# The layer norm's subtract-and-scale on GpSimd instead of VectorE, in a four-layer fp32 attention kernel

## Chip, cores and metric

One Trainium2 chip, one core. The metric is the device time of one execution in microseconds (us). Everything is fp32.

## What is computed

The input x has 8 sequences of 112 rows of 256 values (896 rows); the context has 8 sequences of 375 rows of 192. Four layers follow on each other, ten stages in all:

- L0 and L1: self-attention (16 heads of 64), cross-attention to the context (16 heads of 64), and a gated feed-forward of inner width 1024.
- L2: one cross-attention (16 heads of 64).
- L3: causal self-attention (16 heads of 16), cross-attention (16 heads of 16), feed-forward.

Ahead of each stage stands a layer norm, and after it a residual sum:

```python
def _layer_norm(x, g, b):
    m = jnp.mean(x, axis=-1, keepdims=True)
    v = jnp.mean(jnp.square(x - m), axis=-1, keepdims=True)
    return (x - m) * jax.lax.rsqrt(v + EPS) * g + b
...
h = _layer_norm(x, g, b); x = x + stage(h) @ Wo + bo
```

There are ten norms over 896 rows. The part `(x - m) * rsqrt(v + EPS)` is what the change moves; `g` and `b` are applied later, when the transposed result is copied out of PSUM.

## The kernel before

The residual x lies in SBUF as seven tiles of 128 rows by 256 (`x_sb`; the profile merges them as `x`, and a norm's result as `xn`). The work on TensorE (PE) is cut into items with a cost and a due time. A planner (class `Plan`) emits them one after the other: the attention steps are the backbone, and projections, output products, transposes of normed tiles and feed-forward blocks are filled in between by due time. PE's order is written out by this planner and is kept as it is (`manual_schedule` for PE alone). The other engines' orders are set by the tile framework from the same program; each engine runs its own queue in order, so that an instruction that waits holds all that is behind it.

An attention step s (function `add_step`) does for four heads (cross) or eight or sixteen (self):

1. `emit_s`: scores on PE into PSUM (L818).
2. `softmax`: in L3's self-attention VectorE (DVE) adds the causal mask (L777); DVE takes the row maximum with a minus sign (`nm`, L783; L787 caps it in L3); ScalarE (ACT) takes exponentials and their sums (`pr`, L793); DVE takes the reciprocal (`rinv`, L799 and L803); GpSimd (POOL) multiplies `pr` by it (L800 for each cross-attention head, 112x375; L804 for eight self-attention heads at once, 112x896).
3. `emit_t`: PE transposes `pr` (L837), and a copy takes it out of PSUM into `wT`.
4. `emit_pv`: PE multiplies `wT` with the values (L857), and a copy brings the result into `oT`.

The order in PE's queue is scores of step i+2, values product of step i, then the transposes of step i+1 with filler items between them.

Copies out of PSUM go through `evac` (L299 to L303 on ACT, L307 to L311 on DVE). It keeps a running load of ACT and of DVE and gives each copy to the one that would be done first; `busy(engine, us)` adds to this load what other instructions take. It changes which engine copies, not PE's order. PSUM has four buffers for these tiles (`mm`), and PE waits for a copy where all four are held.

The output product of a stage (`add_products`) ends with DVE adding PSUM to the residual tile (L553), after which `norm` is called at once for the next stage:

- DVE: `bn_stats` (L498), `bn_aggr` (L500, mean and variance into `mv`), the variance plus EPS (`ve`, L502).
- POOL: `ve` to the power -0.5, giving `rs` (L504, 128x1).
- DVE: `xn = (x - mean) * rs` (L506, 128x256).
- POOL: the next stage's bias row is added to the residual tile (L507, 128x256), once xn has read it.

The small tiles `st`, `mv`, `ve` and `rs` have four buffers each and xn has three; a buffer is free again when its last reader is done. Some time later PE transposes xn (L520, function `add_norm_transposes`), for tiles two at a time, and two copies apply `g` and `b`.

`norm` is called 70 times: seven at the start of the program, and 63 times spread over the other stages. What else is in POOL's queue: at the start the memset of `brows`, a DMA into it (L344), its scaling (L345) and a memset (L346), which PE's transpose of `brows` (L349) waits for; near the end of L2 the context mask (`ctxB`, L481, 1x3000) and memsets of padded weights (L426, L434, L444, L454); in L3 memsets of the spread value tiles (L624), which DVE then fills (L625). The sync engine's queue (SP) issues the loads of weights and rows.

Of the kernel before, what the change touches and what calls it, by code (L numbers as in the profile page):

```python
# [12 lines left out]
ALU = mybir.AluOpType  # L13
# [249 lines left out]
def kernel(ctx: ExitStack, tc: tile.TileContext, a: dict, out: bass.AP):  # L263
    nc = tc.nc
# [23 lines left out]
    def busy(eng, us):  # L288
        load[eng] = max(load[eng], plan.now) + us
# [27 lines left out]
    for t in range(NT):  # L317
        xt = const.tile([P, D], F32, name=f"x{t}")
# [176 lines left out]
    def norm(st, t):  # L495
        xt = x_sb[t]
        s6 = small.tile([P, 6], F32, tag="st", name="st")
        nc.vector.bn_stats(s6, xt)  # L498
        mv = small.tile([P, 2], F32, tag="mv", name="mv")
        nc.vector.bn_aggr(mv, s6)  # L500
        ve = small.tile([P, 1], F32, tag="ve", name="ve")
        nc.vector.tensor_scalar_add(ve, mv[:, 1:2], EPS)  # L502
        rs = small.tile([P, 1], F32, tag="rs", name="rs")
        nc.gpsimd.tensor_tensor(rs, ve, mhalf, ALU.pow)  # L504
        xn = xpool.tile([P, D], F32, tag="xn", name="xn")
        nc.vector.tensor_scalar(xn, xt, mv[:, 0:1], rs, ALU.subtract, ALU.mult)  # L506
        nc.gpsimd.tensor_add(xt, xt, got[("row", st)])  # L507
        busy("dve", 1.3)
        xns[(st, t)] = xn

    def add_norm_transposes(st, g, bt, deadline, first=False):
# [29 lines left out]
    def add_products(st, nxt, w, n, after, deadline):  # L541


        for t in range(NT):

            def fn(t=t):
                ps = mm_tile()
                for c in range(n):
                    nc.tensor.matmul(  # L549
                        ps[:, :D], lhsT=oT[:, c, t * P : (t + 1) * P], rhs=got[w][:, c, :],  # L550
                        start=(c == 0), stop=(c == n - 1),
                    )
                nc.vector.tensor_add(x_sb[t], ps[:, :D], x_sb[t])  # L553
                busy("dve", 0.42)
                if nxt is None:
                    nc.sync.dma_start(oflat[t * P : (t + 1) * P, :], x_sb[t])
                else:
                    norm(nxt, t)

            plan.add(  # L560
                Item(
                    ("out", t) if nxt is None else ("norm", nxt, t), n * 0.43, fn, deadline(t),
                    uses=[w] + ([] if nxt is None else [("row", nxt)]), deps=after(t),
                    seg=SEG[st] + (info[st][0] == "ff"),
                )
            )
# [591 lines left out]
    for t in range(NT):  # L1158
        norm(0, t)
        plan.refs[("row", 0)] = plan.refs.get(("row", 0), 0)  # L1160
        plan.ev[("norm", 0, t)] = 1.0
# [67 lines left out]
```

## Time before, and its profile

| | us |
|---|---|
| median of 3 runs | 1764.25 |
| lowest and highest run | 1763.3 and 1764.34 |
| the profiled execution's own time | 1763.93 |
| its span | 1762.1 |
| PE busy in the span | 1698.7 |
| POOL busy | 821.6 |
| DVE busy | 894.7 |
| ACT busy | 760.4 |
| xn on DVE (L506), 70 instructions, median of one | 0.412 |
| rs on POOL (L504), 70 instructions, median of one | 0.567 |
| row add on POOL (L507), 70 instructions, median of one | 0.726 |
| DVE idle ahead of xn until rs came, in total | 71.1 |

A profile is of one execution. A line of its timeline reads: start in us from the span's start, duration, engine, line of the kernel, operation, output<-input, shape, count; in square brackets the time that the engine stood idle before it and the instruction whose end released it. PE is the matrix engine, PEld its weight loads, which overlap PE. A line of the table by stage gives for each stretch of the span the busy time of the engines, and in brackets the number of instructions. A wait for several events is put down to the one that came last.

The stretches that matter below: 0 to 20 us is the start (x is loaded, the first norm, its transposes); up to about 1080 run L0 and L1, up to about 1397 L2, up to about 1485 L3's self-attention, up to about 1706 L3's cross-attention, and the rest is L3's feed-forward. The borders overlap, since each stage's projections and the last products of the one before are filled in between steps.

### The profile page before, as it was taken

What the parts mean: (1) busy time and instruction counts of PE and PEld (TensorE: products, weight loads), DVE (VectorE), ACT (ScalarE), POOL (GpSimd) and SP (SyncE); (2) the same over time, 40 slices, a digit from 0 to 9 for tenths busy, and PEclk for the clock granted to TensorE, in tenths of its full rate; (3) what the DMA queues carried; (4) which work ended last, traced back from release to release, by engine and by line L of the source; (5) the groups of instructions that cost most, each with busy time, mean ns of one, the idle gap of its engine ahead of it and who ended that gap; (6) DMA issues with size and microseconds to landing.
All of it is one profiled execution on the core that took longest, in us unless ns stands there. A gap on an engine that the chain in (4) does not pass through costs nothing.

```text
span 1762.1 us, 30334 instructions
## 1 busy us (share of the span) xinstructions
PE 1698.7 (96%) x11886; PEld 1187.1 (67%) x11886; DVE 894.7 (51%) x2106; ACT 760.4 (43%) x2420; POOL 821.6 (47%) x755
## 2 busy tenths in 40 slices
PE   6999999999999999999999999999999888999979
PEld 5777666666658876666666657766656776666656
DVE  2454455455522445555455523555555477666640
ACT  3553344444412444344444421444444356555541
POOL 3212545455601222555455602645657535788860
PEclk9999999999999999999999999999999999999999
DMA  6012011000101110000000100100000101000000
GB/s 182 4 48 52 3 29 54 25 1 1 49 28 42 28 49 25 1 28 1 25 1 1 43 27 9 10 1 1 7 1 7 11 14 50 2 1 1 1 1 22
DMA packets 39464, 39.12 MB, mean 22 GB/s; under 512 B 16928, under 2 KB 34568, under 8 KB 39321
## 3 DMA queue, kind: packets, MB, share of 16 engines
q1 hardware_dynamic: 39257, 37.13, 7.6%
q8 instruction: 94, 1.54, 0.4%
q14 instruction: 49, 0.40, 0.1%
q0 software_dynamic: 64, 0.05, 0.0%
HBM read 35.48 MB, written 0.92 MB: 21 GB/s over the span
## 4 chain that ended last, share of the span: by engine, by line
PE 85%; DVE 5%; POOL 4%; ACT 4%; issue 1%; DMA 0%; SPq 0%; ACTq 0%; POOLq 0%; DVEq 0%
PE mm L581 11%; PE mm L549 11%; PE mm L837 9%; PE s L818 9%; PE mm L857 9%; PE mm L677 7%; PE mm L1030 7%; PE mm L643 7%; PE mm L686 4%; PE mm L652 4%; PE mm L605 3%; ACT pr L793 3%; POOL pr L800 3%; DVE nm L783 2%; PE mm L707 1%; PE mm L728 1%
## 5 line engine op out<-in xcount | busy, mean ns | idle before, releaser
L800 POOL TENSOR_SCALAR pr<-pr,rinv 112x375 f32<-112x375 f32 x512 | 623.9, 1238 | 400.3 <-DVE rinv L799 394.1
L793 ACT ACTIVATE pr<-s,nm 112x375 f32<-112x375 f32 (+1 forms) x768 | 374.2, 503 | 260.9 <-DVE nm L783 171.5
L783 DVE TENSOR_REDUCE nm<-s 112x2 f32<-112x750 f32 (+1 forms) x288 | 266.1, 952 | 63.9 <-PE s L818 59.8
L837 PE MATMUL mm<-ident,pr 112*128 112x112 f32 (+2 forms) x1920 | 240.9, 264 | 17.8 <-DVE oT L311 5.9
L837 PEld LDWEIGHTS mm<-ident,pr 112*128 112x128 f32 (+2 forms) x1920 | 213.3, 151 | 64.1 <-issue 15.7
L303 ACT COPY wT<-mm 128x448 f32<-128x448 f32 (+2 forms) x292 | 153.0, 535 | 179.1 <-PE mm L837 178.6
L857 PEld LDWEIGHTS mm<-wT,v 128*64 128x64 f32 (+5 forms) x3840 | 161.7, 130 | 94.1 <-issue 33.6
L857 PE MATMUL mm<-wT,v 128*64 128x112 f32 (+5 forms) x3840 | 202.4, 266 | 15.7 <-ACT wT L303 12.3
L818 PE MATMUL s<-kT,qT 64*112 64x375 f32 (+3 forms) x1792 | 208.6, 394 | 0.0
L804 POOL TENSOR_TENSOR pr<-pr,rinv 112x896 f32<-112x896 f32 x48 | 80.8, 1684 | 267.9 <-DVE rinv L803 248.0
L818 PEld LDWEIGHTS s<-kT,qT 64*112 64x112 f32 (+1 forms) x1792 | 113.5, 173 | 68.3 <-issue 15.6
L793 ACT ACTIVATION_READ_ACCUMULATOR pr<-s,nm 112x1 f32 x768 | 158.3, 206 | 0.0
L799 DVE RECIPROCAL rinv<-sums 112x1 f32<-112x1 f32 x512 | 83.1, 162 | 98.6 <-ACT pr L793 88.4
L311 DVE COPY kT<-mm 128x375 f32<-128x375 f32 (+1 forms) x117 | 65.6, 561 | 119.0 <-PE mm L652 99.9
L311 DVE COPY wT<-mm 128x448 f32<-128x448 f32 (+2 forms) x188 | 114.2, 611 | 14.0 <-PE mm L837 11.0
L311 DVE COPY v<-mm 128x512 f32<-128x512 f32 (+2 forms) x75 | 51.8, 691 | 130.2 <-PE mm L686 109.5
L303 ACT COPY kT<-mm 128x375 f32<-128x375 f32 (+1 forms) x107 | 51.2, 478 | 128.3 <-PE mm L652 115.2
L504 POOL TENSOR_TENSOR rs<-ve,mhalf 128x1 f32<-128x1 f32 x70 | 39.2, 561 | 143.9 <-DVE ve L502 142.0
L553 DVE TENSOR_TENSOR x<-mm,x 128x256 f32<-128x256 f32 x70 | 29.4, 419 | 128.7 <-PE mm L549 128.6
L643 PE MATMUL mm<-ctxA,L_xattn_Wk 128*128 128x375 f32 x256 | 91.7, 480 | 0.0
L677 PE MATMUL mm<-L_xattn_Wv,ctxA 128*128 128x512 f32 (+1 forms) x192 | 90.7, 595 | 0.4 <-ACT hT L299 0.4
L303 ACT COPY v<-mm 128x512 f32<-128x512 f32 (+2 forms) x53 | 31.1, 586 | 125.6 <-PE mm L686 120.4
(130 smaller groups left out, 2342.2 us busy)
## 6 DMA issues: line engine op xcount, KB each, us to landing
L_xattn_Wq<-in_L_xattn_Wq_dram SPq DMA_DIRECT2D x3, 1024.0 KB, 6.8
L_xattn_Wo<-in_L_xattn_Wo_dram SPq DMA_DIRECT2D x3, 1024.0 KB, 15.2
L_xattn_w_ff<-in_L_xattn_w_ff_dram SPq DMA_DIRECT2D x3, 1024.0 KB, 5.7
L_xattn_Wp<-in_L_xattn_Wp_dram SPq DMA_DIRECT2D x2, 1024.0 KB, 7.5
L_xattn_wq<-in_L_xattn_wq_dram SPq DMA_DIRECT2D x2, 1024.0 KB, 4.9
L_xattn_wo<-in_L_xattn_wo_dram SPq DMA_DIRECT2D x2, 1024.0 KB, 5.8
L_xattn_mlp_w<-in_L_xattn_mlp_w_dram SPq DMA_DIRECT2D x2, 1024.0 KB, 4.9
cn<-in_ctx_dram SPq DMA_DIRECT2D x2, 843.8 KB
```

The lines of the kernel that those rows point to most:

```text
L303: nc.scalar.copy(dst, src)
L311: nc.vector.tensor_copy(dst, src)
L549: nc.tensor.matmul(ps[:, :D], lhsT=oT[:, c, t * P : (t + 1) * P], rhs=got[w][:, c, :], start=(c == 0), stop=(c == n - 1),)
L581: nc.tensor.matmul(ps[:, i * 2 * T : (i + 1) * 2 * T], lhsT=got[w][:, k, m * P : (m + 1) * P], rhs=hT[:, k, lo:hi], start=(k == 0), stop=( ...
L643: nc.tensor.matmul(ps[:, :S], lhsT=got[w][:, (2 * u + i) * P : (2 * u + i + 1) * P], rhs=ctxA[:, cols], start=True, stop=False,)
L677: nc.tensor.matmul(ps[: KCH[c][1], :], lhsT=lhs(ctxA, slice(0, KA), c), rhs=got[w][:, hf * 512 : (hf + 1) * 512], start=True, stop=False,)
L783: nc.vector.tensor_reduce(nm[:, :, :ns], sv, AX.X, ALU.max, negate=True)
L793: nc.scalar.activation(pr[:, bk, sl, :], sv[:, bk, sl, :], AF.Exp, bias=nm[:, bk, sl : sl + 1], accum_out=sums[:, bk, sl : sl + 1],)
L800: nc.gpsimd.tensor_scalar_mul(pr[:, bk, sl, :], pr[:, bk, sl, :], rinv[:, bk, sl : sl + 1])
L818: nc.tensor.matmul(tiles[i][:, n % 2, (n // 2) * nk : (n // 2 + 1) * nk], lhsT=qap(h), rhs=kap(h), start=True, stop=True,)
L837: nc.tensor.transpose(pt[:kl, i * T : (i + 1) * T], cell[h][:, c * P : c * P + kl], ident[:T, :T])
L857: nc.tensor.matmul(po[p0 : p0 + dp, blk * T : (blk + 1) * T], lhsT=got[vk][:kl, hv * dp : (hv + 1) * dp], rhs=wt, start=(c == 0), stop=(c ...
```

## The change

The instruction that makes xn is issued on GpSimd's queue, between the power that gives `rs` and the row add, instead of on VectorE's. The load figure that `evac` is told for a norm's instructions on VectorE goes from 1.3 to 0.8. Nothing else is edited.

```diff
@@ -503,9 +503,9 @@
         rs = small.tile([P, 1], F32, tag="rs", name="rs")
         nc.gpsimd.tensor_tensor(rs, ve, mhalf, ALU.pow)
         xn = xpool.tile([P, D], F32, tag="xn", name="xn")
-        nc.vector.tensor_scalar(xn, xt, mv[:, 0:1], rs, ALU.subtract, ALU.mult)
+        nc.gpsimd.tensor_scalar(xn, xt, mv[:, 0:1], rs, ALU.subtract, ALU.mult)
         nc.gpsimd.tensor_add(xt, xt, got[("row", st)])
-        busy("dve", 1.3)
+        busy("dve", 0.8)
         xns[(st, t)] = xn
```

In the built program 70 instructions move from VectorE's queue to GpSimd's. PE's queue and SP's keep their order. Ten of some 1300 copies out of PSUM go to VectorE instead of ScalarE.

## The prediction

> **What bounds the kernel now.** I read part 1 of the page, then the busy time by stage, then the waits of VectorE (DVE) and of TensorE (PE), and last the timeline wherever PE stands still.
>
> ```profile
> PE 1698.7 (96%) x11886; PEld 1187.1 (67%) x11886; DVE 894.7 (51%) x2106; ACT 760.4 (43%) x2420; POOL 821.6 (47%) x755
> ```
>
> PE is the bound: it idles 63 us of a span of 1762.1. The stages show where (start:end, then length, PE, weight loads, DVE, ACT, POOL, clock, DMA):
>
> ```profile
> 0.00:40.00 40.00, 25.00 (x123) 21.45 (x124) 9.73 (x33) 12.86 (x34) 11.54 (x26) 1.00 0.62 183
> ...
> 20.00:1355.00 1335.00, 1330.00 (x8765) 914.42 (x8764) 647.73 (x1445) 552.64 (x1725) 568.37 (x495) 1.00 0.08 22
> 1355.00:1397.00 42.00, 36.64 (x264) 29.77 (x266) 18.30 (x51) 14.18 (x39) 30.87 (x30) 0.96 0.18 12
> 1397.00:1485.00 88.00, 77.14 (x813) 63.83 (x806) 69.99 (x150) 52.27 (x261) 32.68 (x35) 0.96 0.10 30
> 1485.00:1706.00 221.00, 197.21 (x1820) 138.41 (x1817) 144.16 (x415) 124.69 (x370) 176.17 (x168) 0.98 0.01 2
> ```
>
> From 20 to 1355 us PE idles 5 us in all: whatever VectorE loses there on GpSimd (POOL) is hidden. Time can be won or lost in the first 20 us, and in block L3 from 1355 to 1706, where PE idles 40 us (5.4 + 10.9 + 23.8).
>
> The wait that the change aims at is this one, of DVE (total, times, longest):
>
> ```profile
> DVE xn L506 <- POOL rs L504: 71.1, 60, 8.5
> ```
>
> Of it, 39.3 us in 19 waits lie after 1355. The worst, and a usual one in the cross attention of L3:
>
> ```profile
> 1357.66 7.78 POOL L481 TENSOR_SCALAR ctxB<-c 1x3000 f32<-1x3000 uint8 x1 [0.17 <-POOL x L507]
> ...
> 1373.32 0.57 POOL L504 TENSOR_TENSOR rs<-ve,mhalf 128x1 f32<-128x1 f32 x1
> 1373.93 0.41 DVE L506 TENSOR_SCALAR xn<-x,mv,rs 128x256 f32<-128x256 f32 x1 [8.52 <-POOL rs L504]
> ...
> 1375.66 1.76 PE L857 MATMUL mm<-wT,v 119*64 119x112 f32 x16 [5.36 <-ACT wT L303]
> ...
> 1514.46 0.57 POOL L504 TENSOR_TENSOR rs<-ve,mhalf 128x1 f32<-128x1 f32 x1
> 1515.07 0.41 DVE L506 TENSOR_SCALAR xn<-x,mv,rs 128x256 f32<-128x256 f32 x1 [2.33 <-POOL rs L504]
> 1515.40 0.93 DVE L783 TENSOR_REDUCE nm<-s 112x2 f32<-112x750 f32 x1
> 1515.56 0.73 POOL L507 TENSOR_TENSOR x<-x,row 128x256 f32<-128x256 f32 x1 [0.53 <-DVE xn L506]
> 1517.61 4.88 POOL L800 TENSOR_SCALAR pr<-pr,rinv 112x375 f32<-112x375 f32 x4 [1.32 <-DVE nm L787]
> ```
>
> DVE stands at xn while POOL works off its queue; the evictions and row maxima behind xn are late, then ACT, then PE. At 1514 it costs POOL too: it idles 0.53 us for xn and 1.32 for maxima that DVE could have started at 1513.1, when the scores were there.
>
> [...] here (1683 - 726) / (896 - 256) = 1.50 (L804 against L507), so I price from rows. [...] 4.88 / 4 = 1.22 us for L800, agreeing with its 1.238.
>
> **The price of xn on POOL, X.** No such row exists. POOL's one-operation TENSOR_SCALARs are L345 (128 elements, 0.542 us) and L800 (375, 1.238): slope 2.82 ns, rest 0.18, so 0.90 for 256. I take 0.95 for the second operation and the semaphore. Low end 0.73, the L507 add of this shape; high end 1.62, if the second operation doubles the slope (0.18 + 256 x 5.64).
>
> **1. The start: +3.9 us.** PE's first transposes stand behind the brows transpose, which POOL releases.
>
> ```profile
> 10.80 2.07 POOL L507 TENSOR_TENSOR x<-x,row 128x256 f32<-128x256 f32 x3 [3.54 <-DMA L_xattn_Wq<-in_L_xattn_Wq_dram]
> ...
> 15.18 0.28 PE L349 MATMUL mm<-ident,brows 16*128 16x16 f32 x1 [10.83 <-POOL brows L346]
> ...
> 16.12 2.43 DVE L506 TENSOR_SCALAR xn<-x,mv,rs 128x256 f32<-128x256 f32 x4 [0.45 <-PE mm L520]
> ...
> 19.09 2.30 PE L581 MATMUL mm<-hT,L_xattn_Wq 128*128 128x224 f32 x8
> ```
>
> In POOL's new order two xn precede the row add that waits until 10.80 (free: POOL idles 3.54 us there), the third precedes brows: +0.95, so PE starts at 16.15. The other four need xn buffers (three exist) that PE frees from about 17.1, and two row adds of 0.7 stand among them: 17.1 + 4 x 0.95 + 1.4 = 22.3, where DVE ended the last at 18.55. So +3.75, with semaphores between POOL instructions +3.9. This wait of xn for PE blocks POOL's row adds, which nobody needs yet. Five X count: 5X - 0.85. PE is saturated afterwards, so this stays to the end. DVE's bn_aggr now waits for POOL to free mv (four buffers) at tiles 4 to 6; the rs of those tiles runs behind the row adds anyway.
>
> **2. 1355 to 1485: -7.8 us.** (a) At 1365.4 DVE goes on at once; ACT's wT copy, behind a qT that waited for DVE, comes about 1369 instead of 1375.1, and the 5.36 of PE go. The next transposes need only the L800 that ended at 1372.3. POOL runs xn and the add until 1375.9, before its next rinv, at 1376.96, was due: free. (b) At 1410 DVE waits 1.24 for rs, then 0.33 of xn, ahead of L777; PE stands 2.50 at 1415 for the copy behind it. L777 starts at 1409.2 when its scores are there: -1.5. (c) At 1423 the same, bounded by the scores at 1423.15: -0.9, kept because DVE and ACT run in turn until 1467. (d) At 1466 the 2.49 us give nothing: PE waits there for exponentials that end at 1466.1 anyway, and is then busy until 1477.
>
> **3. 1485 to 1706: -5.1 us.** From pow to the next L800 now takes 3.15 us (1514.46 to 1517.61). After: 0.57 + X + 0.72 and three gaps of about 0.07 (L346 starts 0.06 after L345) = 1.51 + X; DVE's maxima run during the preceding L800, off the path. Gain 1.64 - X = 0.69. Six tiles do this (1514, 1566, 1621, 1671, 1689, 1697): -4.1. At 1522 three memsets stand between: 3.67 against 2.32 + X: -0.4. The pair at 1679 and 1681 takes 5.43 against 2 x (1.45 + X) + 0.06: -0.6. At 1574 PE is busy until 1582, and at 1705 the feed-forward follows: nothing.
>
> **4. Costed at nothing.** In 20 to 1355 POOL is busy 43%; per tile it works X and no longer waits 0.53. If that cover went, 50 tiles x 0.42 would be 21 us at most. xn's transposes follow xn by 0.82 us or more, except at 1127 and 1523: a few tenths, against as many won from the 5 us. The smaller busy value (0.8 for 1.3) moves ten of about 1300 PSUM copies from ACT to DVE, five of them after 1485, 0.6 us each on a DVE at 65%. PE's order and SP's are unchanged, and no DMA moves; L624's memsets and L481 keep their place behind the adds.
>
> **Sum.** +3.9 - 7.8 - 5.1 = -9.0 on the profiled execution's 1763.93 (span 1762.1, 1.8 around it; the runs' median is 1764.25, 0.3 more): about **1755 us**, -0.5%. By X, the parts add up to 14X - 22.3: -12 at 0.73, 0 at 1.59.
>
> **Rivals.**
> - Two operations take two passes (X = 1.62): +0.4, **1764.3**. For it: L800's 2.82 ns an element already looks like a loop bound by its operations. Against: nothing shown has two. 12%.
> - Slower: POOL becomes the bound of L3's cross attention and the start is drawn out. It decides from X = 1.84 (+3.5); at X = 2.0, +5.7, **1769.6**. Needs the second operation to more than double the slope[...]. POOL's 80% busy there speaks for it, X's bounds against. 10%.
> - Only the stop at 1370 counts; elsewhere DVE waits in turn for PE, ACT or POOL's pr buffers (L777), so that the change doesn't free DVE as it says: 3.9 - 5.4 = -1.5, **1762.4**. For it: PE is 89% busy after 1485. 8%.
> - More: the PE stalls behind late DVE copies next to norms after 1485 (some 13 us of the 23.8) go almost wholly, POOL's delay lying under them: -7.8 - 12 + 3.9, **1748**. 10%.
>
> **How the numbers follow.** The forecast, 1755 (1749 to 1760), has 60%. Low 1746 takes in the last rival, high 1766 the first and third; about 15% lie outside. The measurement tells about 0.2%, 3.5 us, from no change. Faster: 60 + 10, and 2 of the third; same 18; slower 10.
>
> **What would show it.** xn on POOL at 0.9 to 1.0 us; the wait of xn for rs gone; the first L581 at 22 to 23 us; no 5 us hole near 1375; pow to next L800 in 2.4 to 2.6 instead of 3.15; PE idle between 1485 and 1706 near 19. X over 1.5, or new PE waits for xn, would make it wrong.

## The result, and the profile after

| | before | changed |
|---|---|---|
| median | 1763.28 us (6 runs, 1762.21 to 1764.34) | 1757.22 us (6 runs, 1755.20 to 1757.64) |
| profiled execution (span) | 1763.93 (1762.1) | 1756.80 (1755.0) |

The ratio is 0.9962, 95% interval 0.9951 to 0.9972: 6.7 us less (4.9 to 8.6). The two profiled executions are 7.1 us apart. What the sum of the prediction gave is 9.0.

Part 1 of the page after: TensorE (PE) is still the bound, GpSimd (POOL) has 85 us more to do, VectorE (DVE) 20 us less.

```profile
PE 1696.6 (97%) x11886; PEld 1186.7 (68%) x11886; DVE 874.6 (50%) x2046; ACT 756.1 (43%) x2410; POOL 906.6 (52%) x825
```

The busy time by stage, changed kernel (start:end, then length, PE, weight loads, DVE, ACT, POOL, clock, DMA). The same clock times aren't the same work: at 1365 the changed kernel is 9.8 us behind.

```profile
0.00:40.00 40.00, 20.90 (x85) 17.46 (x86) 6.84 (x27) 7.92 (x14) 19.81 (x33) 1.00 0.56 180
20.00:1355.00 1335.00, 1325.47 (x8705) 910.65 (x8706) 628.13 (x1392) 549.41 (x1715) 618.01 (x537) 1.00 0.08 22
1355.00:1397.00 42.00, 41.30 (x288) 33.58 (x285) 19.25 (x54) 16.34 (x46) 37.95 (x35) 1.00 0.21 18
1397.00:1485.00 88.00, 78.48 (x848) 66.09 (x846) 71.81 (x152) 52.73 (x260) 42.58 (x45) 0.98 0.10 31
1485.00:1706.00 221.00, 202.48 (x1876) 142.06 (x1869) 145.13 (x414) 126.12 (x372) 190.32 (x180) 0.98 0.01 2
```

In the first 40 us PE idles 19.1 us instead of 15.0, and from 20 to 1355 9.5 instead of 5: losses. From 1355 to 1397 it idles 0.7 us instead of 5.4, and from 1485 to 1706 18.5 instead of 23.8: gains. DVE's wait for `rs`, 71.1 us before, is gone; PE has two new waits on POOL (total, times, longest, from 20 us on):

```profile
PE mm L520 <- POOL xn L506: 12.5, 8, 3.2
PE mm L837 <- POOL pr L800: 5.2, 8, 0.9
```

To see where the time went I matched the 70 norms of the two traces by their variance instruction (L502) and took the difference of the starts. It stays constant over long stretches, and moves in few places:

| stretch, by the clock of before | prediction | changed against before |
|---|---|---|
| start to 137 | +3.9 (step 1) | +6.09 |
| 137 to 1121 | 0 (step 4) | -0.95 |
| 1121 to 1365 | 0 (step 4) | +4.64 |
| 1365 to 1387 | -5.4 (step 2a) | -7.07 |
| 1387 to 1422 | -2.4 (steps 2b, 2c) | -2.28 |
| 1422 to 1513 | 0 (step 2d) | -0.19 |
| 1513 to 1715 | -5.1 (step 3) | -7.36 |
| sum | -9.0 | -7.12 |

**The start.** Timeline of the changed kernel:

```profile
16.02 0.28 PE L349 MATMUL mm<-ident,brows 16*128 16x16 f32 x1 [11.23 <-POOL brows L346]
...
17.03 2.42 POOL L506 TENSOR_SCALAR xn<-x,mv,rs 128x256 f32<-128x256 f32 x2 [1.07 <-PE mm L520]
...
20.82 2.41 POOL L506 TENSOR_SCALAR xn<-x,mv,rs 128x256 f32<-128x256 f32 x2
...
23.29 0.69 PE L520 MATMUL mm<-ident,xn 128*128 128x128 f32 x2 [0.51 <-POOL xn L506]
23.77 3.19 PE L581 MATMUL mm<-hT,L_xattn_Wq 128*128 128x224 f32 x8
```

`brows` comes 0.84 us later, and each of the last four xn takes 1.2 us on POOL, with two row adds between. The first projection (L581) starts at 23.77 instead of 19.09.

**The start of L2.** The prediction put nothing down for this place. Before, where PE waited 0.42 us for xn:

```profile
1125.85 2.65 POOL L800 TENSOR_SCALAR pr<-pr,rinv 112x375 f32<-112x375 f32 x2 [3.21 <-DVE rinv L799]
1126.51 0.90 DVE L506 TENSOR_SCALAR xn<-x,mv,rs 128x256 f32<-128x256 f32 x2
...
1126.97 0.93 PE L520 MATMUL mm<-ident,xn 128*128 128x128 f32 x4 [0.42 <-DVE xn L506]
...
1129.13 1.76 PE L581 MATMUL mm<-hT,L_xattn_Wq 128*128 128x224 f32 x8
```

Changed kernel:

```profile
1127.20 0.57 POOL L504 TENSOR_TENSOR rs<-ve,mhalf 128x1 f32<-128x1 f32 x1
...
1130.98 2.45 POOL L800 TENSOR_SCALAR pr<-pr,rinv 112x375 f32<-112x375 f32 x2 [3.21 <-DVE rinv L799]
...
1133.42 2.44 POOL L506 TENSOR_SCALAR xn<-x,mv,rs 128x256 f32<-128x256 f32 x2
1134.70 0.29 PEld L520 LDWEIGHTS mm<-ident,xn 128*128 128x128 f32 x2 [3.26 <-POOL xn L506]
1134.70 0.69 PE L520 MATMUL mm<-ident,xn 128*128 128x128 f32 x2 [3.02 <-POOL xn L506]
...
1137.89 3.04 PE L581 MATMUL mm<-hT,L_xattn_Wq 128*128 128x224 f32 x8
```

The last two tiles' power is done by 1127.8, but their xn have no buffer until PE's transposes at 1130.81 to 1131.7 free some; POOL stands idle up to 1130.98. Then two rescalings (L800) are ahead of both xn in POOL's queue, and each xn takes 1.22 us. Before, DVE did both (0.45 us each) while POOL did those rescalings. PE stands 3.02 us, and then the eight matmuls of L581 take 3.04 us where before they took 1.76.

**The stop at 1370** is gone. Changed kernel:

```profile
1368.26 7.78 POOL L481 TENSOR_SCALAR ctxB<-c 1x3000 f32<-1x3000 uint8 x1
...
1375.99 1.69 PE L581 MATMUL mm<-hT,L_xattn_qkv_w 128*128 128x224 f32 x8
...
1378.13 0.53 ACT L303 COPY wT<-mm 119x448 f32<-119x448 f32 x1 [1.00 <-PE mm L837]
...
1383.94 0.57 POOL L504 TENSOR_TENSOR rs<-ve,mhalf 128x1 f32<-128x1 f32 x1
...
1384.62 1.23 POOL L506 TENSOR_SCALAR xn<-x,mv,rs 128x256 f32<-128x256 f32 x1
```

L481 still holds POOL, the power and xn still come behind it, but DVE doesn't stand there any more and the copies ahead of L857 come in time.

**L3's cross-attention.** POOL in the changed kernel:

```profile
1683.77 0.57 POOL L504 TENSOR_TENSOR rs<-ve,mhalf 128x1 f32<-128x1 f32 x1
1684.45 1.23 POOL L506 TENSOR_SCALAR xn<-x,mv,rs 128x256 f32<-128x256 f32 x1
1685.77 0.72 POOL L507 TENSOR_TENSOR x<-x,row 128x256 f32<-128x256 f32 x1
1686.46 4.88 POOL L800 TENSOR_SCALAR pr<-pr,rinv 112x375 f32<-112x375 f32 x4
1691.31 0.57 POOL L504 TENSOR_TENSOR rs<-ve,mhalf 128x1 f32<-128x1 f32 x1
```

From the power to the next L800 it is 2.69 us instead of 3.15. POOL has hardly a gap left: a step with a norm takes 7.54 us of it, from power to power.

**The clock behind a stop.** The clock column of windows of 4 us shows what the stops cost on top. Before, at the stop of 1370:

```profile
1372.00:1376.00 4.00, 0.34 (x4) 0.34 (x6) 2.07 (x5) 1.22 (x3) 2.47 (x7) 0.93 0.27 21
1376.00:1380.00 4.00, 4.00 (x26) 3.62 (x23) 1.81 (x7) 2.33 (x8) 3.04 (x3) 0.65 0.00 0
```

And the changed kernel at its new stop:

```profile
1132.00:1136.00 4.00, 0.77 (x3) 0.38 (x4) 1.09 (x3) 0.91 (x3) 4.00 (x5) 0.72 0.02 4
1136.00:1140.00 4.00, 4.00 (x16) 3.82 (x17) 1.03 (x2) 1.45 (x3) 3.69 (x4) 0.50 0.11 33
```

PE is busy all through the second window of each, at 0.65 and 0.50 of its clock. In the clock records that the column averages, every spell of these two traces up to 1715 us is at 0.50, and it lasts 3.41 us, or 6.83 like the one at the new stop (1133.78 to 1140.61). Half a clock over 3.41 us is 1.7 us lost, and (1 - 0.57) x 4 = 1.7 us is what the column shows from 1416 to 1420 before (clock 0.57), and in the windows at 1468, 1676 and 1700 after. Before has six such spells (behind the stops at 1375, 1415, 1467, 1575, 1685 and 1701), 10.1 us in all, counted as half of PE's busy time in them; the changed kernel has four, 7.8 us.

In the 3.41 us ahead of each of these ten spells PE was busy for 0 to 52% of the time (0% at 1375, 34% at 1416, 39% at the new stop, 52% at 1700 in the changed kernel). The reverse doesn't hold: before, PE was busy for 52% from 1433.45 to 1436.86, and the clock was 1.00 in the 3.41 us behind it. What decides it the traces don't show.

### The profile page after: what moved, and what is told of

Its sections match the earlier page's. It is cut to its first block, busy times and chain, and to the rows that moved or that the text cites. A ratio compares the mean times of both kernels' runs of the same rounds, so it can differ in the third digit from the quotient of the medians.

```text
span 1755.0 us, 30348 instructions
## 1 busy us (share of the span) xinstructions
PE 1696.6 (97%) x11886; PEld 1186.7 (68%) x11886; DVE 874.6 (50%) x2046; ACT 756.1 (43%) x2410; POOL 906.6 (52%) x825
## 4 chain that ended last, share of the span: by engine, by line
PE 85%; POOL 6%; ACT 4%; DVE 4%; issue 1%; DMA 0%; SPq 0%; ACTq 0%; POOLq 0%; DVEq 0%
PE mm L581 11%; PE mm L549 11%; PE mm L837 9%; PE s L818 9%; PE mm L857 9%; PE mm L677 7%; PE mm L643 7%; PE mm L1030 7%; PE mm L686 4%; PE mm L652 4%; POOL pr L800 4%; PE mm L605 3%; ACT pr L793 3%; DVE nm L783 2%; POOL xn L506 1%; PE mm L728 1%
## 5 line engine op out<-in xcount | busy, mean ns | idle before, releaser
L800 POOL TENSOR_SCALAR pr<-pr,rinv 112x375 f32<-112x375 f32 x512 | 623.5, 1236 | 366.2 <-DVE rinv L799 362.8
L857 PEld LDWEIGHTS mm<-wT,v 128*64 128x64 f32 (+5 forms) x3840 | 160.3, 129 | 84.6 <-issue 32.5
L857 PE MATMUL mm<-wT,v 128*64 128x112 f32 (+5 forms) x3840 | 200.1, 264 | 7.4 <-ACT wT L303 4.5
L799 DVE RECIPROCAL rinv<-sums 112x1 f32<-112x1 f32 x512 | 83.4, 163 | 98.7 <-ACT pr L793 88.1
L311 DVE COPY wT<-mm 128x448 f32<-128x448 f32 (+2 forms) x195 | 118.6, 612 | 21.3 <-PE mm L837 18.2
L506 POOL TENSOR_SCALAR xn<-x,mv,rs 128x256 f32<-128x256 f32 x70 | 85.8, 1226 | 7.7 <-PE mm L520 1.1
```

What stands on the lines that cost most here:

```text
L311: nc.vector.tensor_copy(dst, src)
L800: nc.gpsimd.tensor_scalar_mul(pr[:, bk, sl, :], pr[:, bk, sl, :], rinv[:, bk, sl : sl + 1])
L857: nc.tensor.matmul(po[p0 : p0 + dp, blk * T : (blk + 1) * T], lhsT=got[vk][:kl, hv * dp : (hv + 1) * dp], rhs=wt, start=(c == 0), stop=(c ...
```

## The experiments

Each was run beside the kernel before, whose medians lay between 1762.48 and 1763.15 us. Where a kernel has lines more than the original, its own line numbers are a few higher; the text keeps to those of before.

### The start on VectorE (start_dve)

```diff
-        nc.gpsimd.tensor_scalar(xn, xt, mv[:, 0:1], rs, ALU.subtract, ALU.mult)
+        on_pool = st > 0
+        eng = nc.gpsimd if on_pool else nc.vector
+        eng.tensor_scalar(xn, xt, mv[:, 0:1], rs, ALU.subtract, ALU.mult)
-        busy("dve", 0.8)
+        busy("dve", 0.8 if on_pool else 1.3)
```

> The change, but the seven norms of the start keep xn on VectorE. Theory A (the trace's own account: the first projection of the changed kernel starts 4.7 us later, and TensorE works another 1.4 us slower in what follows): 1757.2 - 6.1 = 1751.1 us, first L581 back at 19.1. Rival (only the late start counts, and the slow matmuls after it have another cause): 1752.5. Rival (the start is made up later by waits for weights anyway): 1757.

Measured: 1750.52 us, ratio 0.9927 (0.9915 to 0.9939), 6.7 us under the changed kernel. The start's cost is 6 to 7 us, not 3.9 or 4.7: theory A. The stop of 3.02 us at the start of L2 is in its trace as well, and costs 4.0 there.

### GpSimd for L3's norms alone (l3_only)

The same edit with `on_pool = st >= 7`.

> xn on GpSimd only for the three norms of L3 (21 of 70), on VectorE before. Theory A (losses lie before 1361 us, gains after it: the two traces are 9.8 us apart at 1361 one way and 7.1 the other way at the end): 1763.3 - 16.9 = 1746.4 us. Rival (the gains are what the prediction summed, 7.8 + 5.1, and the rest of what the trace shows is the later clock): 1750.4. Rival (L3's gain depends on the order that the earlier stages leave behind): over 1753.

Measured: 1749.09 us, ratio 0.9922 (0.9910 to 0.9934). The losses are gone: against the kernel before its norms run 1.2 us earlier from 137 us up to 1365, unchanged. The gain, 13.8 us, lies between A's 16.9 and the rival's 12.9. In its trace 1365 to 1387 gives -7.1 and 1387 to 1422 -2.3 as in the changed kernel, 1422 to 1513 +1.5 (the clock records have a spell behind a stop at 1424 that the other two traces lack, and one at 1456 that is 6.83 us long where theirs are 3.41) and 1513 to 1715 -5.9 instead of -7.4.

### One xn of 70 (hole_only), and L481 elsewhere (mask_only)

hole_only has `on_pool = (st, t) == (7, 2)`. mask_only is the kernel before, with

```diff
-            nc.gpsimd.tensor_scalar_mul(ctxB[KB : KB + 1, :], c8[KB : KB + 1, :], NEG)
+            nc.scalar.activation(ctxB[KB : KB + 1, :], c8[KB : KB + 1, :], AF.Copy, scale=NEG)
```

> One xn of 70 on GpSimd: the one of the tile whose power sits behind the context mask L481. Theory A (the stop of TensorE at 1370 to 1375.7 goes, and with it the low clock of 0.65 over the 4 us that follow it, 1.4 us): 1763.3 - 6.9 = 1756.4 us. Rival, as in the prediction (the stop alone): 1757.9. Rival (what comes next is late anyway): 1761 or more.

> The kernel before, every xn on VectorE, with the context mask L481 on ScalarE instead of GpSimd and nothing else changed. It measures the stop at 1370 by itself, of which hole_only's median kept less than its trace. Theory A (the stop with the low clock behind it, 7.1 us): 1763 - 7.1 = 1756 us, and no stop over 1 us between 1360 and 1390. Rival (part of it comes back later, as the median of hole_only has it): 1759.

Measured: hole_only 1759.27 us (1755.02 to 1760.41), ratio 0.9971 (0.9961 to 0.9982); mask_only 1755.17 us, ratio 0.9963 (0.9950 to 0.9977). Both traces show -7.1 from 1365 to 1387, as the changed kernel does. hole_only's median keeps 4 us: its runs at 1759 and more have a mean clock of 0.991 or 0.992, those at 1755 one of 0.993 or 0.994, which points to other spells of low clock; but the run at 1757.23 has 0.995, so the clock isn't all of it. What differs in the runs without a trace stays open. mask_only settles the stop: one instruction on another engine, every xn still on VectorE, and the time is that of the whole change. mask_only's timeline:

```profile
1368.52 0.57 POOL L504 TENSOR_TENSOR rs<-ve,mhalf 128x1 f32<-128x1 f32 x1
...
1369.12 0.41 DVE L506 TENSOR_SCALAR xn<-x,mv,rs 128x256 f32<-128x256 f32 x1 [2.89 <-POOL rs L504]
...
1370.52 1.38 PE L857 MATMUL mm<-wT,v 128*64 128x112 f32 x24
```

VectorE still waits for the power, 2.89 us instead of 8.52, and PE doesn't notice. L481 takes 2.70 us on ScalarE instead of 7.78. The stop of 2.50 us at 1415 is still there (at 1408.97), but no low clock follows it this time, and 1387 to 1422 comes out 1.7 us shorter for it. PE is busy for 2.47 of the 4 us from 1404 on and for 3.03 of the next 4, and the column reads 1.00 from 1392 to 1440; before, PE was busy for 1.50 of the 4 us from 1412 on, and 0.57 followed. Why the clock fell behind the one and not behind the other isn't shown.

### The load figure (load_old)

```diff
-        busy("dve", 0.8)
+        busy("dve", 1.3)
```

> The change without its second line: xn on GpSimd, but each norm still counts 1.3 us as VectorE's load, so that copies are shared out as before. Theory A (the ten copies that change sides cost and bring nothing): 1757.2 within 1 us. Rival (the gain in L3 comes in part from copies that VectorE now takes over from ScalarE): 1759 or more.

Measured: 1754.05 us (1753.75 to 1757.13), ratio 0.9956 (0.9943 to 0.9969), against 0.9962 (0.9951 to 0.9972) for the change. Its median is 3.2 us lower than the change's, but the intervals overlap widely; it also lies outside theory A's 1 us. The second line of the diff brings no gain; whether it costs a few us isn't settled.

### The price of xn on GpSimd (price)

```diff
+        m = mv[:, 0:1]
+        if t == 0:
             nc.gpsimd.tensor_scalar(xn, xt, m, rs, ALU.subtract, ALU.mult)
+        elif t == 1:
+            nc.gpsimd.tensor_scalar(xn, xt, m, None, ALU.subtract)
+        elif t == 2:
+            nc.gpsimd.tensor_scalar(xn, xt, 0.5, 2.0, ALU.subtract, ALU.mult)
+        elif t == 3:
+            nc.gpsimd.tensor_scalar(xn, xt, 2.0, None, ALU.mult)
...
+        elif t == 5:
+            nc.gpsimd.tensor_scalar(xn, xt, rs, None, ALU.mult)
...
```

> The seven tiles of every stage take xn in seven forms, to price it; all but tiles 0, 4 and 6 leave out or replace part of the norm's subtract-and-scale. Tile 0: as in the change (1.23 us). Tile 1: subtract alone, tile 5: scale alone, each with one per-partition operand. Tile 2: both operations with constants. Tile 3: scale by a constant. Tile 4: both operations, in two halves of 128 columns. Tile 6: on VectorE. Theory A (the second operation is what the prediction's 0.95 left out): tiles 1, 3 and 5 at 0.85 to 0.95, tile 2 at 1.2. Rival B (the per-partition operands cost): tiles 2 and 3 at 0.9, tiles 1 and 5 near 1.05. Rival C (the line through L345 and L800 is wrong for 256 columns, whatever the form): all whole tiles near 1.2.

Measured, in the groups of POOL by shape (busy us, mean ns):

```profile
L518 POOL TENSOR_SCALAR xn<-x,mv,rs 128x128 f32<-128x128 f32 x20 | 15.9, 798 | 1.0
L508 POOL TENSOR_SCALAR xn<-x,mv,rs 128x256 f32<-128x256 f32 x10 | 12.3, 1228 | 1.0
L512 POOL TENSOR_SCALAR xn<-x 128x256 f32<-128x256 f32 x10 | 10.8, 1084 | 2.1 <-DVE x L569 2.0
L520 POOL TENSOR_SCALAR xn<-x,rs 128x256 f32<-128x256 f32 x10 | 9.3, 931 | 0.8
L510 POOL TENSOR_SCALAR xn<-x,mv 128x256 f32<-128x256 f32 x10 | 9.3, 928 | 2.7 <-DVE mv L500 2.7
L514 POOL TENSOR_SCALAR xn<-x 128x256 f32<-128x256 f32 x10 | 8.6, 861 | 2.2 <-DVE x L569 1.1 <-PE mm L536 1.0
```

One operation with a per-partition operand is 0.93 (the prediction's line through L345 and L800 had given 0.90), with a constant 0.86. The second operation adds 0.22 (1.084 against 0.861), and each per-partition operand 0.07: 0.86 + 0.22 + 2 x 0.07 = 1.22. Theory A named the larger part (though its tile 2 was to take 1.2), rival B the rest; C falls.

### Four buffers for xn (ring4)

```diff
-    xpool = ctx.enter_context(tc.tile_pool(name="xpool", bufs=3))
+    xpool = ctx.enter_context(tc.tile_pool(name="xpool", bufs=4))
...
-        ve = small.tile([P, 1], F32, tag="ve", name="ve")
-        nc.vector.tensor_scalar_add(ve, mv[:, 1:2], EPS)
+        nc.vector.tensor_scalar_add(mv[:, 1:2], mv[:, 1:2], EPS)
...
-        nc.gpsimd.tensor_tensor(rs, ve, mhalf, ALU.pow)
+        nc.gpsimd.tensor_tensor(rs, mv[:, 1:2], mhalf, ALU.pow)
```

> The change with four buffers for xn instead of three (room made by adding EPS in place, without the tile ve). Theory A (at 1131 us TensorE waits 3.0 us since the sixth and seventh xn get their buffers only when three others have been transposed, and then stand on GpSimd's queue; one more buffer lets the sixth start at once): that wait falls under 2 us, the low clock after it goes, the start gains 1 us; 1757.2 - 4.3 = 1752.9 us. Rival (the two rescalings L800 that stand ahead of xn and xn's own 1.23 us make the wait, not the ring): 1757.

Measured: 1756.33 us (1752.96 to 1759.63), ratio 0.9957 (0.9944 to 0.9971): no change that can be told. The sixth xn, which now has a buffer, does start at once (1120.18). The seventh still has none when its power is done:

```profile
1128.62 0.57 POOL L503 TENSOR_TENSOR rs<-mv,mhalf 128x1 f32<-128x1 f32 x1
...
1132.22 1.09 PE L519 MATMUL mm<-ident,xn 128*128 128x128 f32 x8
...
1132.39 2.45 POOL L799 TENSOR_SCALAR pr<-pr,rinv 112x375 f32<-112x375 f32 x2 [3.20 <-DVE rinv L798]
...
1134.83 1.23 POOL L505 TENSOR_SCALAR xn<-x,mv,rs 128x256 f32<-128x256 f32 x1
...
1136.12 0.69 PE L519 MATMUL mm<-ident,xn 128*128 128x128 f32 x2 [2.80 <-POOL xn L505]
```

It gets its buffer from the transposes at 1132.22, stands behind two L800 (here L799) and ends at 1136.06; PE waits 2.80 us, and a low clock follows (the mean clock of this run is 0.994, of the changed kernel's 0.995). Theory A's wait of under 2 us didn't come, and the time is nearer the rival's. But this doesn't clear the ring: POOL stood idle for 3.20 us ahead of those L800, and an xn with a buffer could have run there. The wait is made by the late buffer, the queue and xn's length together; whether five buffers would end it wasn't run.

### The power left out (no_pow)

```diff
-        nc.gpsimd.tensor_tensor(rs, ve, mhalf, ALU.pow)
+        nc.vector.reciprocal(rs, ve)
```

> The kernel before with the reciprocal of the variance in place of its power -0.5, taken on VectorE: the norm's power is left out, and with it every wait of VectorE for GpSimd, while xn stays on VectorE. Theory A (what the change gains is the wait for the power; what it loses is xn's time on GpSimd's queue): all gains and no losses, 1763.3 - 7.1 - 2.3 - 7.4 = 1746.5 us or less; less, down to 1737, if GpSimd is what bounds L3's cross-attention, since each norm then takes 0.7 of it there and not 2.7. Rival (the gain in L3 comes from the order, not from the wait or from GpSimd's load): 1750 or more.

Measured: 1738.04 us, ratio 0.9861 (0.9847 to 0.9874). This is what it is worth when VectorE doesn't wait for the power and GpSimd does neither the power nor xn: 24 us, 3.6 times what the change gets. It lies near the 1737 that theory A gives for GpSimd as the bound; the rival falls.

### GpSimd relieved (l3_relief, relief_dve, relief_st7, relief_mask)

```diff
-                    nc.gpsimd.tensor_scalar_mul(pr[:, bk, sl, :], pr[:, bk, sl, :], rinv[:, bk, sl : sl + 1])
+                    if not (dh == 16 and n == 0):
+                        nc.gpsimd.tensor_scalar_mul(pr[:, bk, sl, :], pr[:, bk, sl, :], rinv[:, bk, sl : sl + 1])
                     busy("dve", 0.16)
+            if nch > 1 and dh == 16:
+                nc.scalar.activation(pr[:, 0, 0, :], pr[:, 0, 0, :], AF.Copy, scale=rinv[:, 0, 0:1])
+                busy("act", 0.47)
```

A step's four heads come as two pairs, so this moves two of its four rescalings to ScalarE, not one as I wrote for l3_relief. l3_relief is l3_only with this edit; relief_dve is the kernel before with it; relief_st7 has xn on GpSimd for the norm ahead of L3's self-attention alone; relief_mask is relief_dve with mask_only's edit.

> As l3_only (xn on GpSimd for L3's three norms alone), and in L3's cross-attention one of the four rescalings L800 of each step goes to ScalarE. Theory A (from 1640 us on GpSimd is the bound: its steps with a norm follow each other at 7.54 us with hardly a gap): those steps come to 6.3 us, and the time falls by 4 to 8 us from l3_only's 1749.1, to 1743. Rival (TensorE waits there for copies of ScalarE and VectorE, and GpSimd is only late beside them): 1749 or more.

> The kernel before (every xn on VectorE) with the same rescalings of L3's cross-attention on ScalarE as in l3_relief, which takes two of each step's four. It tells what xn on GpSimd is worth once GpSimd no longer bounds L3's cross-attention. Theory A (of the change's gains the stop at 1370 with its low clock, 7.1 us, and the next ones to 1431, 2.3 us, stay lost; in the cross-attention nothing is left to gain): 1726.7 + 9.4 = 1736 us, within 2. Rival (VectorE's wait for the power costs in the cross-attention by itself): 1740 or more. Rival (with GpSimd relieved xn is better on VectorE there): under 1733.

> As l3_relief, but xn on GpSimd for the norm ahead of L3's self-attention alone (seven of 70), on VectorE for the two after it. Theory A (those two gain nothing once GpSimd is relieved): 1726.7 us within 2. Rival (VectorE's wait for the power is a cost of its own in the cross-attention): 1730 or more. Rival (GpSimd still bounds the steps with a norm): under 1724.

> As relief_dve, every xn on VectorE, and the context mask L481 on ScalarE instead of GpSimd. Theory A (the stop at 1370 comes from the power waiting behind L481 in one queue, and not from VectorE's doing xn): the stop goes without the change, 1736 - 7.1 = 1729 us, less the part of L481 that ScalarE now holds. Rival (another wait of VectorE for GpSimd takes its place): 1734 or more.

| kernel | xn of L3's norms on | median, us | ratio (95%) |
|---|---|---|---|
| relief_dve | VectorE | 1744.60 | 0.9891 (0.9877 to 0.9906) |
| relief_mask | VectorE, L481 on ScalarE | 1736.96 | 0.9852 (0.9836 to 0.9869) |
| relief_st7 | GpSimd for the first, VectorE for two | 1737.25 | 0.9850 (0.9835 to 0.9865) |
| l3_relief | GpSimd | 1726.73 | 0.9796 (0.9782 to 0.9809) |

l3_relief, the best of all, is 22.4 us under l3_only, much more than theory A's 4 to 8. The busy times of the same stretch of L3 (1629 matmuls in both), first l3_only:

```profile
1504.00:1700.00 196.00, 178.73 (x1629) 125.44 (x1626) 127.72 (x365) 108.19 (x313) 168.76 (x162) 0.97 0.01 1
```

then l3_relief:

```profile
1504.00:1676.00 172.00, 169.11 (x1629) 121.07 (x1630) 130.09 (x386) 124.69 (x350) 101.06 (x105) 1.00 0.01 2
```

POOL falls from 86% to 59% busy, PE rises from 91% to 98%, and the clock column from 0.97 to 1.00. So GpSimd did bound the cross-attention of L3, as theory A says, over all of it and not just from 1640 on.

For relief_dve theory A had 1736 and for relief_st7 1726.7: both fell, and the numbers of the rival that VectorE's wait costs by itself came. relief_st7 against l3_relief says what xn on GpSimd is worth for the two later norms when GpSimd has room: 10.5 us. In the two traces 8.4 us of it lie in L3's cross-attention, and 1.7 are a spell of low clock at 1464 in relief_st7 (mean clock 0.998, of l3_relief 0.999). The pair moves two things at once, the wait and the 0.41 us of each xn; no run parts them. DVE's waits in L3's cross-attention in relief_dve (l3_relief has none of this line):

```profile
DVE xn L506 <- POOL rs L504: 10.2, 11, 1.3
```

With two L800 in front of the power instead of four, the wait is at most 1.3 us and no longer 2.6. relief_mask against relief_dve gives 7.6 us, the stop at 1370 once more; relief_st7 against relief_dve 7.4.

## Why the prediction was right, and where it wasn't

The sign and the size came out, 1755 against 1757.2, but two errors stand against each other: losses up to 1365 us that were missed (9.8 against 3.9) and gains after it that were priced too low (16.9 against 12.9). That the number came so close is in part luck.

**X, the price of xn on POOL.** 0.95 was taken; L506 took 1.21 to 1.25 us. As a price of one operation it is right (0.93); the 0.05 for the second operation and the semaphore was the mis-sized term: 0.22 for the operation, and 0.14 for two per-partition operands (part of one is in the line through L800 already). Against VectorE, xn takes 1.227 / 0.412 = 3.0 times as long on POOL. "By X, the parts add up to 14X - 22.3" gives -5.1 for 1.227; measured 6.7 to 7.1.

**Step 1, the start.** Mechanism right: 5X - 0.85 at 1.227 is 5.3, the first L581 came 4.7 later. Left out: PE's clock just after. The traces' clock records begin at 20.33 us before and at 27.86 changed; ahead of them the clock column prints 1.00 without having a record. I estimate with half a clock up to there, the 0.50 of the later spells: PE then loses half of its work between the first L581 and the first record, half of 1.24 us before and half of 4.09 changed. The sum is 4.68 + 2.05 - 0.62 = 6.11, and 6.09 was measured at 137 us. The estimate also fits the first eight L581: 3.19 us changed, 2.30 before, 1.69 later on (1375.99). The start itself varies: kernels with the old start stand at -1.4 to +1.0 at 137 us, so its cost is 6 within 1.

**Step 2.** (a) had the right wait and the right place; the term that it lacked is the low clock behind the stop: 5.36 + 1.7 = 7.1, measured 7.07 in the changed kernel and in the eleven experiments' traces that lack the stop. (b) and (c) were 2.4 together and came to 2.3, by another way than written: from 1387 to 1409 0.98 us is lost, and then the stop at 1415 falls from 2.50 to 1.00 and its low clock doesn't come, 3.3 in all. (d) came to -0.2, as expected.

**Step 3.** The way from the power to the next L800 is 2.69 instead of 2.46 us, from X alone (1.51 + 1.23 = 2.74), so that a tile gains 0.46 and not 0.69; six give 2.8. Yet the stretch gained 7.4: from the norm at 1513 to the one at 1715 PE idles 5.3 us less, and loses 1.7 us less to low clock (three spells of 5.1 us in all before, two of 3.4 after). That PE's idle time, 18.5 us from 1485 to 1706, came to the 19 that was named is in part luck, since POOL's shorter chain gives only some 3 us of it. "DVE's maxima run during the preceding L800, off the path" counted only this chain. The relief runs show the other half: xn on VectorE with its wait costs 10.5 us by itself where POOL has room. So the rival "more" had a real gain in view, but in the change POOL, full in that stretch, doesn't let it out: no_pow and l3_relief, which unload POOL, go well below its 1748. I can't split the rest of the idle time between the waits.

**Step 4 is the one that failed.** "xn's transposes follow xn by 0.82 us or more, except at 1127 and 1523: a few tenths" had found the place. It priced xn as if it started when it did before and only took longer. But on POOL, once a buffer for it comes free, it stands behind two L800 that VectorE had worked beside: 2.45 + 1.22 us, a stop of 3.02, and a low clock (0.50 for 6.83 us): +4.6 us. l3_only, which leaves these norms on VectorE, doesn't have it; what part the ring of buffers has in it, ring4 leaves open. The -0.95 lies between 469 and 494, and it is a small gain of the wait: before, VectorE waits 0.92 us for the power at 469, its oT copy is late, PE stands 0.46 us for that copy at 473.04, and the first L1030 starts 1.85 us after the transposes (L520); in the changed kernel it is 0.94. The four other kernels with xn on GpSimd there share the gain (-0.9), no_pow has -0.7, and those with VectorE's wait left in have none. The ten copies show no gain (load_old).

**The rivals.** Two passes, X = 1.62, and GpSimd at X = 2.0, fell with the measured 1.23; no part of the traces is as slow as these wanted. "Only the stop at 1370 counts" has the right main part, and mask_only reaches the change's time with it alone. But the equal times hide that the change gains 17 us from 1365 on (9.8 + 7.1) and loses 9.8 before.

## What to carry to other kernels

An instruction moved to another engine starts not when its input is ready but when that engine's queue and a free buffer let it (at the start of L2 TensorE stood 3.02 us for it), so price for each place what stands ahead of it there; do it everywhere the consumer follows within a few us, also where the engine is half idle. Move it only in the stages that gain: here the same edit in 21 of 70 places is worth 14 us instead of 6.7. And if the engine that takes the work is then as busy in that stage as GpSimd was here (86% from 1504 to 1700 in l3_only), take something off it: that was worth another 22 us, three times the change.

## What the runs showed of the hardware

- A stop of TensorE can cost more than its length. Before and in the changed kernel the clock falls to 0.50 for 3.41 us, in one case 6.83, which costs 1.6 to 1.7 us of PE's work, or 2.7. It fell behind stops of 2.48 to 5.36 us, and behind rows of shorter ones: 2.09, 1.37 and 0.62 (before, at 1685), 2.15, 0.62 and 0.55 (before, at 1702), 0.84, 0.89 and 0.90 (changed kernel, at 1698). It didn't behind a stop of 2.50 us in mask_only (at 1408.97), nor behind the same stop in relief_mask, where PE was busy for 1.50 of the 4 us from 1404 on and the clock column reads 1.00 up to 1412. From 30 to 1120 us, where PE is busy for 1086 of 1090 us in both traces, the clock is 1.00.
- L787, a small VectorE instruction (112x2 or 112x8, median 0.17 us before), took longer at some places where a GpSimd instruction ran beside it: before, at 1495.36, 1508.12, 1542.69, 1559.57, 1595.94 and 1614.81, it took 0.32 to 0.44 us and ended 0.02 to 0.03 us after L624 or L800 did. It doesn't come each time (0.22 at 1504.05, with L800 going on for another 0.64), and what makes L787 longer isn't shown. Over 0.23 us were 11 of the 80 before and 23 in the changed kernel; above 0.165 each, that is 4.4 and 6.6 us of VectorE's time.
- A two-operation tensor_scalar on GpSimd with per-partition operands costs 1.23 us for 128x256 and 0.80 for 128x128: 3.4 ns an element of each partition. The same on VectorE takes 0.41 us.
- The context mask L481, one row of 3000 from uint8 to fp32, took 7.78 us on GpSimd and 2.70 on ScalarE.
